# DVE and ACT in program order, and the softmax's last steps cut into other portions, in a two-layer cross-attention kernel

## The chip, the cores and the metric

The kernel runs on one core of one Trainium2 chip. Its engines work side by side, each through its own queue: TensorE (PE, with its weight loads as PEld), VectorE (DVE), ScalarE (ACT), GpSimd (POOL) and SyncE (SP). POOL and SP here mostly issue DMAs. The metric is the device time of one execution in microseconds (us), as the median of several runs. All data are float32.

## The reference, cut to what matters

Two layers of attention with a residual follow each other; the second takes the first one's output. Each has 8 batches of 100 queries, 640 channels and 20 heads of 32. The context has 722 tokens of 1024 channels per batch: 77 of text, and 645 of the second kind (`ip`). Text and `ip` have weights and a softmax of their own:

```
k, v       = text @ Wk, text @ Wv          # 77 tokens
k_ip, v_ip = ip @ Wk_ip, ip @ Wv_ip        # 645 tokens
out = softmax(q k^T / sqrt(32)) v + softmax(q k_ip^T / sqrt(32) + bias) v_ip * mask
x   = out @ Wo + bo + x
```

In the first layer there is no bias and no mask. In the second, the bias is 0.5 times a "semantic" score that all heads share (a softmax over whole rows of q and k of the text, carried over to the `ip` tokens), and the mask has one number for each query.

## The kernel before, in words

**Units.** The attention is cut into 80 units: 16 batches of a layer (u = 0 to 15, the second layer from 8 on) times 5 chunks of 4 heads (c = 0 to 4). `ORDER` (L41) runs through them batch by batch; for the last pair of batches (14 and 15) it takes chunks 0 and 2 of both, then 1 and 3 of both, then 4 of both. We write (14,3) for batch 14, chunk 3. Keys and values of the `ip` tokens are made two batches (a pair) at a time, by a Strassen-like scheme of seven products (`seven`, L179): PE makes a product in PSUM, ACT or DVE evicts it (L193, L202 on ACT; L198, L208, L213, L219, L224 on DVE). The sums that the scheme needs of the tokens (L232, L233, L527, L543, and L725, L726 for the last pair) and of the weights (L134 to L137) are made on DVE, a few on POOL. The keys and values go to DRAM, and come back for each unit.

**One unit.** `scores(u, c, 0)` makes the scores of 4 heads against the first 512 tokens on PE (L944), `scores(u, c, 1)` those of the other 210, the last 77 of them text. One PSUM tile of four banks holds either; it has no second buffer, so the next scores wait until the last ones have been read. Behind the scores stands the softmax:

- maxima on DVE: L953 in the first layer; in the second L960, which adds the bias, writes the result to `p` and takes the minimum of its negative in one instruction per head;
- exponentials with their sums on ACT (L968), and the text's maxima and its subtraction on DVE (L974, L976), with two small steps on the statistics (L979, L980);
- exponentials of the text and of the correction between the two halves on ACT (L983, L984);
- on DVE the sum over the text's columns (L985), two small steps (L986, L987), the reciprocal (L990) and the factors (L991);
- the scaling of the probabilities `p`: four instructions on ACT, one per head, for the first 512 columns (L997), and two on DVE for the rest (L1005 for the `ip` columns, L1001 for the text's).

One unit later, the probabilities are transposed on PE (`transposes`, L1030: six blocks j = 0 to 5 of four heads each; block 0 reads what L997 wrote), copied from PSUM (L1035 on ACT for j = 2 and 5, L1037 on DVE for the others), and multiplied with the values (`values`, L1052; the result's copy is L1056).

**Portions.** What stands behind the scores is not issued at once. `scores` puts it in portions into the list `later`. Each task of the production of keys and values that has a time of its own in the plan (the first number of its pair, over 0) is followed by one portion (`next_task`, L1220). `free_scores` (L930) issues those that must be out before the scores' PSUM tile is taken again (marked True), and the first transposes of a unit issue all that is left (L1025).

**What sets the order.** The production's tasks are spread over the units by a plan of estimated times (`production`, L1061, and `spread`, L1119), and the loop at L1253 interleaves them with scores, transposes, values, output pieces and query pieces. The whole is traced within `tc.manual_schedule(engines={PE})` (L1211): PE keeps the order in which the program issues its instructions. DVE, ACT and the queues of SP and POOL are ordered by the framework's scheduler, from estimates of its own. On each engine the instructions then run in the order that the build gave them. The start of the kernel (L415, text keys and values) is in a region of its own, where PE alone is pinned.

Of the kernel before, what the change touches and what calls it, by code (L numbers as in the profile page):

```python
# [44 lines left out]
def two_layer_xattn(  # L45
# [407 lines left out]
    def load_q(u):  # L453
        l, b = divmod(u, B)
        t = tpool.tile([P, NC_, S], F32, tag="q", name=f"q_{u}")
        nc.sync.dma_start(t, q_d[l][b // 2][:, b % 2])
        qs_[u] = t

    def load_vt(u):
        l, b = divmod(u, B)  # L460
        t = tpool.tile([NTAIL, C], F32, tag="vt", name=f"vt_{u}")
        nc.sync.dma_start(t[:NL], vl_d[l][b * NL : (b + 1) * NL, :])
        nc.sync.dma_start(t[NL:], vt_d[l][b * NT : (b + 1) * NT, :])
        vts[u] = t
# [459 lines left out]
    later = []  # L924

    def emit(n):
        for _ in range(n):
            later.pop(0)[1]()

    def free_scores():  # L930

        emit(max([i + 1 for i, (r, _) in enumerate(later) if r], default=0))

    def scores(u, c, part):
        k0, k1 = ((0, KA), (KA, NK))[part]
        free_scores()
        if part == 0:
            pr[u, c] = ppool.tile([S, 4, NK], F32, tag="p", name=f"p_{u}_{c}")

            stats[u, c] = stat.tile([S, 14, 4], F32, tag="st", name=f"st_{u}_{c}")  # L940
        sc = ps_sc.tile([P, 4, 512], F32, tag="sc", name=f"sc_{u}_{c}_{part}")
        for i in range(4):
            rows = slice(32 * i, 32 * i + 32)
            nc.tensor.matmul(  # L944
                sc[:S, i, : k1 - k0], lhsT=qs_[u][rows, c, :], rhs=ks[u, c][rows, k0:k1], start=True, stop=True
            )
        p, st, l = pr[u, c], stats[u, c], u // B
        n = min(k1, NI) - k0
        lo, f, rz, mul = st[:, 6, :], st[:, 7:9, :], st[:, 9:11, :], st[:, 11:13, :]

        def maxima(heads):
            if l == 0:
                nc.vector.tensor_reduce(  # L953
                    st[:, part, heads[0] : heads[-1] + 1], sc[:S, heads[0] : heads[-1] + 1, :n], AX.X, ALU.max,
                    negate=True,
                )
                return
            for i in heads:

                nc.vector.tensor_tensor_reduce(  # L960
                    out=p[:, i, k0 : k0 + n], in0=sc[:S, i, :n], in1=sems[u][:, k0 : k0 + n], scale=-1.0,
                    scalar=3.0e38, op0=ALU.add, op1=ALU.min, accum_out=st[:, part, i : i + 1],
                )

        def exponentials(heads):
            for i in heads:
                dst = p[:, i, k0 : k0 + n]
                nc.scalar.activation(  # L968
                    dst, dst if l else sc[:S, i, :n], AF.Exp, bias=st[:, part, i : i + 1],
                    scale=-1.0 if l else 1.0, accum_out=st[:, 3 + part, i : i + 1],  # L970
                )

        def text_maxima():
            nc.vector.tensor_reduce(st[:, 2, :], sc[:S, :, n:KB], AX.X, ALU.max, negate=True)  # L974

            nc.vector.tensor_tensor(  # L976
                p[:, :, NI:], sc[:S, :, n:KB], st[:, 2, :].unsqueeze(2).to_broadcast([S, 4, NT]), ALU.add
            )
            nc.vector.tensor_tensor(lo, st[:, 0, :], st[:, 1, :], ALU.min)  # L979
            nc.vector.tensor_tensor(f, lo.unsqueeze(1).to_broadcast([S, 2, 4]), st[:, 0:2, :], ALU.subtract)  # L980

        def text_exponentials():
            nc.scalar.activation(f, f, AF.Exp)  # L983
            nc.scalar.activation(p[:, :, NI:], p[:, :, NI:], AF.Exp)  # L984
            nc.vector.tensor_reduce(st[:, 5, :], p[:, :, NI:], AX.X, ALU.add)  # L985
            nc.vector.tensor_tensor(st[:, 3:5, :], st[:, 3:5, :], f, ALU.mult)  # L986
            nc.vector.tensor_tensor(st[:, 4, :], st[:, 3, :], st[:, 4, :], ALU.add)  # L987

        def factors():
            nc.vector.reciprocal(rz, st[:, 4:6, :])  # L990
            nc.vector.scalar_tensor_tensor(  # L991
                mul, f, mask_sb[:, l : l + 1], rz[:, 0:1, :].to_broadcast([S, 2, 4]), ALU.mult, ALU.mult
            )

        def scaled(heads):
            for i in heads:
                nc.scalar.activation(p[:, i, :KA], p[:, i, :KA], AF.Copy, scale=mul[:, 0, i : i + 1])  # L997

        def scaled_rest(text):
            if text:  # L1000
                nc.vector.tensor_tensor(  # L1001
                    p[:, :, NI:], p[:, :, NI:], rz[:, 1, :].unsqueeze(2).to_broadcast([S, 4, NT]), ALU.mult
                )
            else:
                nc.vector.tensor_tensor(  # L1005
                    p[:, :, KA:NI], p[:, :, KA:NI], mul[:, 1, :].unsqueeze(2).to_broadcast([S, 4, NI - KA]),
                    ALU.mult,
                )

        if part == 0:  # L1010
            maxima((0, 1))
            later.append((True, lambda: (exponentials((0, 1)), maxima((2, 3)))))
            later.append((True, lambda: exponentials((2, 3))))
        else:
            maxima((0, 1, 2, 3))
            later.append((True, lambda: (exponentials((0, 1, 2, 3)), text_maxima())))
            later.append((False, text_exponentials))
            later.append((False, lambda: (factors(), scaled((0, 1)), scaled_rest(False))))
            later.append((False, lambda: (scaled((2, 3)), scaled_rest(True))))

    pts = {}

# [185 lines left out]
        if n == len(ORDER) - 4:  # L1208
            last_out_weights()

    with tc.manual_schedule(engines={mybir.EngineType.PE}):  # L1211
        for _, f in pair_tasks(PAIRS[0]):
            f()
        load_q(0)
        load_vt(0)
        load_k(0, 0)
        todo = production()
        done = [0]

        def next_task():  # L1220
            todo[done[0]][2]()
            if todo[done[0]][0] and later:
                emit(1)
            done[0] += 1

        def make(until):
            while done[0] < len(todo) and todo[done[0]][1] < until:
                next_task()

        mark = [0]  # L1230

        def apart(until):

            while done[0] < len(todo) and todo[done[0]][1] < until and not any(
                t for t, _, _ in todo[mark[0] : done[0]]
            ):
                next_task()
            mark[0] = done[0]

        def between(n, a, b, small):  # L1240

            mark[0] = done[0]
            near = 0.4 if n < NC_ * LAST[0] + 6 else 0.1
            for i, (_, f) in enumerate(small):
                make(n + a + (b - a) * (i + 1) / (len(small) + 1))
                apart(n + b + near)
                f()
            make(n + b)
            apart(n + b + near)

        make(0.0)
        last = None
        for n, (u, c) in enumerate(ORDER):  # L1253
            at = small_work(n)
            loads(n)
            scores(u, c, 0)
            if n == len(ORDER) - 1:
                load_v(*last)
                load_v(u, c)
            between(n, 0.0, 0.4, at[0])  # L1260
            if last:
                transposes(*last, 0)
                transposes(*last, 1)
            between(n, 0.4, 0.6, at[1])
            if last:
                transposes(*last, 2)
                transposes(*last, 3)
            scores(u, c, 1)
            if n == NC_ * LAST[0] - 1:
                load_q(LAST[1])  # L1270
            between(n, 0.6, 0.8, at[2])
            if n < len(ORDER) - 2:
                load_v(u, c)
            if n + 1 < len(ORDER):
                load_k(*ORDER[n + 1])
            if last:
                transposes(*last, 4)
                transposes(*last, 5)
            between(n, 0.8, 1.0, at[3])
            if last:  # L1280
                values(*last)
            last = (u, c)
        last_out(0, [NC_ - 1])
        for j in range(6):
            transposes(*last, j, at_end=True)
        last_out_add(0)
        values(*last)
        last_out(1, [NC_ - 1])
        last_out_add(1)
# [46 lines left out]
```

## Time and profile before

| | |
|---|---|
| time, median of 3 runs | 2071.55 us (2071.48 to 2073.55) |
| time of the profiled execution | 2071.6 us |
| its span in the profile | 2069.8 us |
| mean granted TensorE clock | 0.998 |
| DMA, over the span | 255.35 MB, 123 GB/s |
| scaling on ACT, L997 | 320 instructions, 713 ns each |
| sum over the text's columns on DVE, L985 | 80 instructions, 469 ns each |
| maxima of the second layer on DVE, L960 | 320 instructions, 489 ns each (512 and 133 columns) |

The profiled execution took the median's time, and its span is 1.8 us less than its time; the rest lies around the program. The busy time of an engine says how full it is, not that it sets the end; for that one reads which engine waited for which (the view of waits) and the chain of work that ended last, followed back from the last instruction. The timeline lists instructions in the order of their start: start, duration, engine, line, operation, tiles and shape, how many in a row, and in brackets how long the engine had been idle and what ended that. PE's weight loads stand as PEld. Tile names come without their numbers, so that `p` may be that of any unit; which unit it is follows from the order.

### The profile page before, as it was taken

What the parts mean: (1) busy time and instruction counts of PE and PEld (TensorE: products, weight loads), DVE (VectorE), ACT (ScalarE), POOL (GpSimd) and SP (SyncE); (2) the same over time, 40 slices, a digit from 0 to 9 for tenths busy, and PEclk for the clock granted to TensorE, in tenths of its full rate; (3) what the DMA queues carried; (4) which work ended last, traced back from release to release, by engine and by line L of the source; (5) the groups of instructions that cost most, each with busy time, mean ns of one, the idle gap of its engine ahead of it and who ended that gap; (6) DMA issues with size and microseconds to landing.
All of it is one profiled execution on the core that took longest, in us unless ns stands there. A gap on an engine that the chain in (4) does not pass through costs nothing.

```text
span 2069.8 us, 38196 instructions
## 1 busy us (share of the span) xinstructions
PE 2043.5 (99%) x15122; PEld 1581.2 (76%) x15122; DVE 1074.8 (52%) x2789; ACT 799.6 (39%) x2271; POOL 309.9 (15%) x445
## 2 busy tenths in 40 slices
PE   9999999999999999999989999999999999999998
PEld 8676767677778777786778777787778778889787
DVE  2211322355554655455475555455555557777676
ACT  1001000244433434344333444435444445565576
POOL 3212312111111111010110111010111111111120
PEclk9999999999999999999999999999999999999999
DMA  9545313232424433262543533262434345545472
GB/s 327 155 132 171 97 56 105 88 107 71 129 83 131 129 113 91 81 179 65 160 133 103 147 105 106 72 178 75 115 89 134 90 133 151 158 133 140 121 211 74
DMA packets 302544, 255.35 MB, mean 123 GB/s; under 512 B 46686, under 2 KB 271378, under 8 KB 302366
## 3 DMA queue, kind: packets, MB, share of 16 engines
q1 hardware_dynamic: 280590, 184.48, 32.2%
q0 software_dynamic: 21776, 68.44, 9.5%
q8 instruction: 119, 1.95, 0.4%
q14 instruction: 59, 0.48, 0.1%
HBM read 183.93 MB, written 68.93 MB: 122 GB/s over the span
## 4 chain that ended last, share of the span: by engine, by line
PE 95%; DVE 2%; DMA 1%; ACT 1%; issue 1%; POOL 0%; SPq 0%; ACTq 0%; DVEq 0%
PE psv_a L597 8%; PE psv_d L597 8%; PE pspt L1030 8%; PE psk_d L625 6%; PE psk_a L625 6%; PE sc L944 6%; PE psk L563 5%; PE psv_e L597 4%; PE pv L1052 4%; PE psv_c L597 4%; PE psv_b L597 4%; PE psk_e L625 3%; PE psk_c L625 3%; PE psk_b L625 3%; PE pso L858 3%; PE psq L275 2%
## 5 line engine op out<-in xcount | busy, mean ns | idle before, releaser
L968 ACT ACTIVATE p<-sc,st 100x512 f32<-100x512 f32 (+1 forms) x320 | 166.4, 528 | 218.5 <-DVE st L953 218.2
L1037 DVE COPY pt<-pspt 128x400 f32<-128x400 f32 x319 | 175.5, 569 | 122.8 <-PE pspt L1030 116.6
L997 ACT ACTIVATE p<-p,st 100x512 f32<-100x512 f32 x320 | 208.5, 713 | 62.8 <-DVE st L991 62.7
L968 ACT ACTIVATE p<-p,st 100x512 f32<-100x512 f32 (+1 forms) x320 | 177.1, 555 | 132.3 <-DVE st L960 131.8
L1030 PEld LDWEIGHTS pspt<-ident,p 100*128 100x128 f32 (+1 forms) x1920 | 188.0, 137 | 42.1 <-issue 5.0
L1030 PE MATMUL pspt<-ident,p 100*128 100x100 f32 (+1 forms) x1920 | 211.0, 250 | 5.7 <-DVE res L863 2.4
L597 PE MATMUL psv_a<-wv,x 128*128 128x397 f32 (+1 forms) x560 | 185.0, 472 | 1.3 <-ACT vo L193 1.3
L646 POOL DMA_DIRECT2D k_d<-ko x140 | 99.5, 715 | 527.6 <-DVE ko L219 470.9
L597 PE MATMUL psv_d<-wv,s 128*128 128x320 f32 (+1 forms) x560 | 174.9, 455 | 0.0
L1035 ACT COPY pt<-pspt 128x400 f32<-128x400 f32 (+1 forms) x161 | 78.4, 487 | 227.7 <-PE pspt L1030 227.3
L953 DVE TENSOR_REDUCE st<-sc 100x2 f32<-100x1024 f32 (+1 forms) x120 | 126.3, 1052 | 59.4 <-ACT p L968 30.5
L597 PEld LDWEIGHTS psv_a<-wv,x 128*128 128x128 f32 x560 | 103.5, 190 | 63.7 <-issue 8.1
L960 DVE CUSTOM_DVE_ANT_0 p<-sc,sem 100x512 f32<-100x512 f32 (+1 forms) x320 | 139.7, 489 | 22.5 <-PE sc L944 22.3
L597 PEld LDWEIGHTS psv_d<-wv,s 128*128 128x128 f32 x560 | 103.4, 190 | 57.4 <-issue 5.5
L625 PE MATMUL psk_a<-x,wk 128*128 128x256 f32 (+1 forms) x672 | 137.2, 350 | 4.2 <-ACT ko L193 4.2
L944 PE MATMUL sc<-k,q 32*100 32x210 f32 (+1 forms) x1280 | 138.6, 502 | 0.8 <-ACT p L968 0.6
L625 PE MATMUL psk_d<-s,wk 128*128 128x256 f32 (+1 forms) x672 | 136.4, 348 | 0.0
L612 POOL DMA_DIRECT2D v_d<-vo x70 | 38.3, 548 | 642.4 <-DVE gst L587 317.5
L563 PE MATMUL psk<-x,wk 128*128 128x256 f32 (+1 forms) x560 | 132.0, 383 | 0.0
L625 PEld LDWEIGHTS psk_a<-x,wk 128*128 128x128 f32 x672 | 110.8, 192 | 24.7 <-issue 6.0
L563 PEld LDWEIGHTS psk<-x,wk 128*128 128x128 f32 x560 | 102.8, 189 | 25.7 <-issue 9.9
L625 PEld LDWEIGHTS psk_d<-s,wk 128*128 128x128 f32 x672 | 108.3, 189 | 17.5 <-issue 5.2
(209 smaller groups left out, 3234.5 us busy)
## 6 DMA issues: line engine op xcount, KB each, us to landing
x<-ip_t SPq DMA_DIRECT2D x84, 512.0 KB
k<-k_d SPq DMA_DIRECT2D x80, 322.5 KB
v<-v_d SPq DMA_DIRECT2D x80, 320.0 KB
v_d<-vo POOLq DMA_DIRECT2D x70, 320.0 KB, 2.5
k_d<-ko POOLq DMA_DIRECT2D x112, 128.0 KB, 4.3
x<-ip_t SPq DMA_DIRECT2D x22, 532.0 KB
o<-wo SPq DMA_DIRECT2D x35, 320.0 KB
q<-wq SPq DMA_DIRECT2D x20, 320.0 KB
```

The lines of the kernel that those rows point to most:

```text
L563: nc.tensor.matmul(ps[:, : 2 * n], lhsT=W["k", 4][:, k, :], rhs=x_all[:, at[j], :, k, :n], start=(k == 0), stop=(k == NCC - 1),)
L597: nc.tensor.matmul(ps[:, :m], lhsT=tokens(k)[:, :P], rhs=w[:, k, :], start=(k == 0 and not go_on), stop=(k == HK - 1), skip_group_check=True,)
L625: nc.tensor.matmul(ps[:, i * m : (i + 1) * m], lhsT=W["k", WHICH[which]][:, k, r * P : (r + 1) * P], rhs=tokens(k), start=(i == 0 and k == ...
L646: nc.gpsimd.dma_start(dst[:, :, r], ko[0][:, h, :, i, p0 : p0 + n])
L944: nc.tensor.matmul(sc[:S, i, : k1 - k0], lhsT=qs_[u][rows, c, :], rhs=ks[u, c][rows, k0:k1], start=True, stop=True)
L953: nc.vector.tensor_reduce(st[:, part, heads[0] : heads[-1] + 1], sc[:S, heads[0] : heads[-1] + 1, :n], AX.X, ALU.max, negate=True,)
L960: nc.vector.tensor_tensor_reduce(out=p[:, i, k0 : k0 + n], in0=sc[:S, i, :n], in1=sems[u][:, k0 : k0 + n], scale=-1.0, scalar=3.0e38, op0= ...
L968: nc.scalar.activation(dst, dst if l else sc[:S, i, :n], AF.Exp, bias=st[:, part, i : i + 1], scale=-1.0 if l else 1.0, accum_out=st[:, 3 ...
L997: nc.scalar.activation(p[:, i, :KA], p[:, i, :KA], AF.Copy, scale=mul[:, 0, i : i + 1])
L1030: nc.tensor.transpose(ps[:rows, i * S : (i + 1) * S], pr[u, c][:, i, j * P : j * P + rows], ident[:S, :S])
L1037: nc.vector.tensor_copy(dst, src)
L1052: nc.tensor.matmul(ps[32 * i : 32 * i + 32, :S], lhsT=lhs, rhs=pt[:rows, j, i * S : (i + 1) * S], start=(j == 0), stop=(j == 5),)
```

## The change

The diff in full:

```diff
@@ -982,11 +982,11 @@
         def text_exponentials():
             nc.scalar.activation(f, f, AF.Exp)
             nc.scalar.activation(p[:, :, NI:], p[:, :, NI:], AF.Exp)
+
+        def factors():
             nc.vector.tensor_reduce(st[:, 5, :], p[:, :, NI:], AX.X, ALU.add)
             nc.vector.tensor_tensor(st[:, 3:5, :], st[:, 3:5, :], f, ALU.mult)
             nc.vector.tensor_tensor(st[:, 4, :], st[:, 3, :], st[:, 4, :], ALU.add)
-
-        def factors():
             nc.vector.reciprocal(rz, st[:, 4:6, :])
             nc.vector.scalar_tensor_tensor(
                 mul, f, mask_sb[:, l : l + 1], rz[:, 0:1, :].to_broadcast([S, 2, 4]), ALU.mult, ALU.mult
@@ -1015,8 +1015,9 @@
             maxima((0, 1, 2, 3))
             later.append((True, lambda: (exponentials((0, 1, 2, 3)), text_maxima())))
             later.append((False, text_exponentials))
-            later.append((False, lambda: (factors(), scaled((0, 1)), scaled_rest(False))))
-            later.append((False, lambda: (scaled((2, 3)), scaled_rest(True))))
+            later.append((False, lambda: (factors(), scaled_rest(False))))
+            later.append((False, lambda: (scaled((0, 1)), scaled_rest(True))))
+            later.append((False, lambda: scaled((2, 3))))
 
     pts = {}
 
@@ -1208,7 +1209,7 @@
         if n == len(ORDER) - 4:
             last_out_weights()
 
-    with tc.manual_schedule(engines={mybir.EngineType.PE}):
+    with tc.manual_schedule(engines={mybir.EngineType.PE, mybir.EngineType.DVE, mybir.EngineType.Activation}):
         for _, f in pair_tasks(PAIRS[0]):
             f()
         load_q(0)
```

DVE and ACT keep the program's order from the first pair's production to the end. The second scores have five portions instead of four: exponentials and text maxima; the text's exponentials; the sum, the factors and L1005; two L997 with L1001; two L997. In the built program, no instruction is added or removed on any engine except waits. PE has its 8,549 matmuls in the same order. On DVE 2,094 of 2,789 instructions stand at another place than before, on ACT 862 of 1,623, on SP's queue 29 of 612, on POOL's 10 of 445; most of them move by a few places. The lines from L985 on shift by two in the new file (L985 to L987, L986 and L987 to L988 and L989), those of `transposes` and `values` by one; the text keeps the line numbers of before where it speaks of before.

## The prediction

> **What bounds the kernel now.** First the page's busy line and the chain that ended last.
>
> ```profile
> PE 2043.5 (99%) x15122; PEld 1581.2 (76%) x15122; DVE 1074.8 (52%) x2789; ACT 799.6 (39%) x2271; POOL 309.9 (15%) x445
> ...
> PE 95%; DVE 2%; DMA 1%; ACT 1%; issue 1%; POOL 0%; SPq 0%; ACTq 0%; DVEq 0%
> ```
>
> TensorE is busy for all but 26 us of 2069.8; DVE and ACT are half idle or more. Reordering them can therefore gain only what TensorE waits for. The view of waits on PE:
>
> ```profile
> PE psk_a L625 <- ACT ko L193: 4.2, 1, 4.2
> ...
> PE psk_c L625 <- DVE ko L198: 1.5, 1, 1.5
> ...
> PE psv_a L597 <- ACT vo L193: 1.3, 1, 1.3
> ...
> PE pspt L1030 <- ACT p L997: 0.3, 1, 0.3
> ```
>
> Beside a start of 4.5 us that the change does not touch, three waits stand out, and the transposes (pspt, L1030) wait for the scaled probabilities (p, L997) for 0.3 us in all. The DVE timeline about the 4.2 us one shows its cause:
>
> ```profile
> 1032.42 0.26 DVE L1056 COPY hs<-pv 128x100 f32<-128x100 f32 x1 [0.71 <-PE pv L1052]
> 1037.67 1.49 DVE L134 TENSOR_TENSOR wvt<-wv,wv 128x1280 f32<-128x1280 f32 x1 [4.98 <-DMA wv<-wvi]
> 1039.08 1.22 DVE L953 TENSOR_REDUCE st<-sc 100x2 f32<-100x1024 f32 x1
> ```
>
> The scheduler put a weight sum (L134) ahead of a score maximum (L953). The sum waited 4.98 us for its DMA, and everything behind it on DVE, then on ACT, then on PE, with it. Last, the timeline of all engines in unit (14,3), where unit (14,1) is finished:
>
> ```profile
> 1997.55 0.46 DVE L985 TENSOR_REDUCE st<-p 100x4 f32<-100x308 f32 x1
> ...
> 1998.88 2.56 ACT L997 ACTIVATE p<-p,st 100x512 f32<-100x512 f32 x4 [0.96 <-DVE st L991]
> ...
> 2000.22 1.12 PE L944 MATMUL sc<-k,q 32*100 32x512 f32 x8
> ...
> 2001.27 2.00 PE L775 MATMUL psk<-x,wk 128*128 128x256 f32 x8
> 2001.40 0.69 DVE L960 CUSTOM_DVE_ANT_0 p<-sc,sem 100x512 f32<-100x512 f32 x1 [0.79 <-PE sc L944]
> 2002.02 0.08 DVE L960 DVE_READ_ACCUMULATOR2_ANT st<- 100x1 f32 x1
> 2002.02 0.69 DVE L960 CUSTOM_DVE_ANT_0 p<-sc,sem 100x512 f32<-100x512 f32 x1
> ...
> 2003.10 0.85 PE L1030 MATMUL pspt<-ident,p 100*128 100x100 f32 x8
> ```
>
> Here the sum over the text columns (L985) starts 3.85 us before the next unit's maxima (L960), and the scaling (L997) ends at 2001.44, 1.9 us before PE reaches the fourth transpose (2003.36). That lead is what the scheduler's freedom buys, and what the change puts at stake.
>
> **The change part by part.** PE's order is the same in both built programs. On DVE and ACT no instruction is added or removed; 36 more wait instructions stand on PE (17 ns each by the row of such waits on ACT, 0.6 us at most, left out).
>
> *The late units.* A unit's portions go out one per timed task, and what is left goes out in one lump ahead of its transposes. There are now seven portions a unit instead of six. A middle pair gives 80 timed tasks to 10 units (8 each); the last pair gives 70 to 14.1 units, 14 to 4 and 6 to 2.05 (5, 3.5 and 3 each, L1105 to L1115). So in the late units the portion with L985 goes out after the next unit's first two maxima, and pinned, it stays there. In (14,3), L985 then starts when the second maximum ends, 2002.71. From L985 to L997 it is 1.33 us (1997.55 to 1998.88), the four L997 take 2.56: they end at 2006.60, and the fourth transpose, due 2003.36, is 3.2 late. Nothing covers it: PE's order is fixed and the next thing in it is the transpose.
>
> The same sum for each unit, with the row that now stands ahead of L985 or L997 (a maximum, or an eviction or copy of a later product) at its time in this trace: (13,4) 2.1; (14,0) 4.3; (14,2) 4.3; (15,0) 3.2; (15,2) 3.2; (14,1) 3.2; (14,3) 5.0; (15,1) 4.1; (15,3) 3.4; (14,4) 3.4. In (15,4) the text maxima (L974) fall behind the copy of (14,4)'s result, which ends at 2057.92; 1.52 us to L985 (2041.34 to 2042.86 in the unit before), 1.33 and 2.56 make 2063.3 against a fourth transpose at 2059.4: 3.9. **Together 40.** Both ends of most of these sums hang on PE's own order, so an earlier stall shifts both and heals nothing; I keep 30 to 44.
>
> *Units (11,3) to (13,3).* The same sum for nine of them gives 0.9 to 2.8 each, 16.7 in all. Here the blocker is mostly an ACT eviction (L193, L202) placed ahead of the scalings. A stall of PE gives ACT time to catch up for the following unit, so I take two thirds: **11** (4 to 17).
>
> *Six earlier units*, (0,3), (2,2), (4,2), (6,1), (6,2), (8,1): one copy of a PE product stands between the second and third L997, and PE goes from that product straight to the transposes. In (0,3): product at its end 482.62, copy L193 from 482.82 for 0.42, two L997 (0.64 apart, 0.71 long) to 484.5; the fourth transpose was due at 482.88: 1.6. **Six times 1.6 is 9.5** (0 to 9.5). The other 54 units have 4.6 to 14 us of lead and lose only lead.
>
> *Other DVE work now late.* The two sums for the last pair's first visit (L232, L233, from 1737.34) come behind two weight sums (1.22 each) and the second softmax's small chain that ends at 1739.4: they end near 1743.1, and PE wants them at 1740.1, 3 us. Three later visits have them behind maxima, 0.7 each. At seven output or query pieces the copy that frees the PSUM buffer (L1037) comes behind a maximum that waits for ACT, about 1 each. **12** (0 to 15).
>
> *What goes.* The weight sums are back behind the work that waits for PE: 4.2, 1.5 and 1.3 go, and with the first the half clock after it, seen here in the windows view (columns: stretch, length, PE, PEld, DVE, ACT, POOL busy, granted clock, DMA, GB/s):
>
> ```profile
> 1036.00:1042.00 6.00, 1.81 (x13) 1.62 (x13) 4.33 (x4) 1.67 (x5) 0.00 (x0) 0.93 0.51 173
> 1042.00:1046.00 4.00, 4.00 (x28) 4.00 (x27) 4.00 (x5) 0.97 (x4) 0.00 (x0) 0.67 0.00 0
> ```
>
> 0.67 over 4 us and 0.93 over 6 are 1.7 us of clock lost. **Minus 8.7** (0 to 8.7).
>
> *Clock.* New stalls may bring new such stretches at 1.7 us each. One followed a 4.2 us wait; the 1.5 and 1.3 us waits brought none; the stretch from 1930 to 1945, with 1.6 us idle in pieces, has a clock of 0.89, again 1.7 lost. Eleven late stalls of 2 to 5 us: 0 to 19; I take three, **5**, because the nearest rows are the single waits.
>
> [...]
>
> *Queues.* On SP 29 of 612 and on POOL 10 of 445 instructions move, by four and eight places at most. The x loads among them are issued two visits ahead, and the POOL sums are wanted only after the products from 207 to 238 us. I cost them at nothing; uncovered, the only landing on the chain is 6.4 us (wv at 1031.22).
>
> Sum: 40 + 11 + 9.5 + 12 - 8.7 + 5 = 69. The profiled execution took 2071.6, the median is 2071.55: **2141 us**.
>
> **Rivals.**
> *Only the late units lose* (the early ones have just enough lead, the sums and copies are absorbed): 40 + 11 - 9 + 0 = 42, about 2114, from 2100 to 2122. For it: a few tenths decide the six early places. Chance 0.16.
> *Every late stall also halves the clock*: 14 us more, 2155 to 2180. For it: the stretch from 1930 to 1945; against it: the waits of 1.5 and 1.3 us that cost no clock. Chance 0.13.
> *Faster:* the three waits and the half clock go, and the late chains arrive in time. 2071.6 - 8.7 is 2063. It decides at one point: the fourth L997 must end before the fourth transpose, so L985 may start later by no more than the lead, 1.9 us in (14,3); by the sum above it starts 5.2 later (1997.55 to 2002.71). It holds only if the portions with L985 go out ahead of those maxima, and the built order has them behind. Chance 0.05.
> *No change*, gains and losses even out within 0.2% (about what a measurement of this kernel can tell): 0.02. A pinning that does not hold is excluded, as the built program has the program's order on both engines.
>
> **How the numbers follow.** My forecast, 2122 to 2155, has 0.62, and 0.02 lies beyond 2180. The range reaches into both slower rivals: 2103 to 2168. Faster 0.05, same 0.02, slower 0.93.
>
> **What would show it.** In the waits on PE: "pspt <- ACT p L997" from 0.3 to about 60 us, most of it after 1930; psk_a and psk_c waits gone; DVE's 4.98 us wait for a DMA ahead of a sum gone. In the late timeline, L985's successor starts just after the second L960. In the windows, the clock stays at 1.00 up to the last units. I am wrong if the transposes' wait stays under 20 us, if it lies in the middle units, or if the lost time shows as a lower clock and not as idle PE.

## The result, and the profile after

The changed kernel takes 2157.02 us (median of six runs, 2155.59 to 2159.99); the kernel before took 2071.52 beside it. The ratio is 1.0414, with a 95% interval of 1.0401 to 1.0427: 85.5 us slower. The profiled execution took 2157.25 us, with a span of 2155.5.

The page of the profile after, in its busy line, its row of the TensorE clock (40 slices of 53.9 us) and its chain:

```profile
PE 2080.6 (97%) x15122; PEld 1600.7 (74%) x15122; DVE 1083.3 (50%) x2789; ACT 796.2 (37%) x2271; POOL 310.0 (14%) x445
...
PEclk9999999999999999999999999999999999999888
...
PE 92%; DVE 4%; ACT 3%; issue 1%; DMA 0%; SPq 0%; ACTq 0%; DVEq 0%
```

PE is idle for 74.9 us (2155.5 less 2080.6) where it was idle for 26.3: 48.6 more. Its busy time grew by 37.1 us with the same 15,122 instructions. So the lost time shows in two ways, and the clock row says where much of it lies: in the last three slices, 162 us, it falls below nine tenths. The waits on PE (us in total, times, longest):

```profile
PE pspt L1031 <- ACT p L997: 44.9, 72, 3.5
PE psvk_b L731 <- DVE sl L233: 5.4, 4, 3.1
PE psq L275 <- DMA wq<-wq: 4.5, 1, 4.5
PE pso L858 <- DVE pt L1038: 3.2, 3, 1.1
```

The transposes' wait for the scaling has risen from 0.3 us to 44.9. The waits named psk_a, psk_c and psv_a, 7.0 us together before, are gone. The timeline of the same place as in the prediction, unit (14,3), in which (14,1) is finished (start, duration, engine, line, and in brackets the idle time before and what ended it):

```profile
2054.26 1.12 PE L944 MATMUL sc<-k,q 32*100 32x512 f32 x8
...
2055.56 0.69 DVE L960 CUSTOM_DVE_ANT_0 p<-sc,sem 100x512 f32<-100x512 f32 x1 [0.89 <-PE sc L944]
...
2056.18 0.69 DVE L960 CUSTOM_DVE_ANT_0 p<-sc,sem 100x512 f32<-100x512 f32 x1
...
2056.79 0.47 DVE L987 TENSOR_REDUCE st<-p 100x4 f32<-100x308 f32 x1
...
2058.12 2.56 ACT L997 ACTIVATE p<-p,st 100x512 f32<-100x512 f32 x4 [0.36 <-DVE st L991]
...
2058.89 0.30 PE L1031 MATMUL pspt<-ident,p 100*128 100x100 f32 x1 [1.59 <-ACT p L997]
...
2059.51 0.30 PE L1031 MATMUL pspt<-ident,p 100*128 100x100 f32 x1 [0.31 <-ACT p L997]
```

The sum over the text's columns (now L987) stands behind the next unit's first two maxima (L960). It starts 2.53 us after the scores, where it started 2.67 ahead of them (1997.55 against 2000.22). L997 follows 1.33 us later and takes 2.56, and PE takes one transpose after each of the four: each L997 releases one.

The windows view of this stretch shows the second part of the loss (columns: stretch, length, PE, PEld, DVE, ACT, POOL busy, granted clock, DMA share, GB/s):

```profile
2054.13:2057.54 3.41, 3.18 (x28) 1.70 (x16) 2.20 (x8) 0.15 (x1) 0.00 (x0) 1.00 0.55 169
2057.54:2060.95 3.41, 1.13 (x5) 0.63 (x6) 2.75 (x8) 3.05 (x6) 1.07 (x2) 1.00 0.72 181
2060.95:2064.37 3.42, 3.42 (x12) 2.88 (x11) 1.15 (x2) 2.55 (x8) 0.00 (x0) 0.50 0.62 171
```

PE works for 1.13 of 3.41 us, and in the next 3.42 us it has work throughout and half the clock (0.50 granted). Before the last matmul such half-clock stretches fill 54.6 us, in twelve places; in the kernel before they fill 6.8 us, in two.

Since both kernels run the same 8,549 matmuls in the same order, the distance between the starts of two neighbours can be compared one by one. What grew is, by the tile that PE was held up at: transposes 63.8 us, matmuls inside half-clock stretches 15.3 (net of those that the kernel before has), the sums' products psvk_b 6.35, output and query pieces and second scores (pso, psq, sc) 10.4; psk_a, psk_c, psv_a and pskt_d give back 8.65. That is 87.2, against 85.7 us of span; 1.5 us of small differences either way stay unassigned. Where to put output pieces that themselves ran at half clock is a choice: counted with the clock, it lost about 17 us, and the pieces and second scores 8.5.

### The profile page after: what moved, and what is told of

It is laid out like the page before. It is cut to its first block, busy times and chain, and to the rows that moved or that the text cites. A ratio compares the mean times of both kernels' runs of the same rounds, so it can differ in the third digit from the quotient of the medians.

```text
span 2155.5 us, 38296 instructions
## 1 busy us (share of the span) xinstructions
PE 2080.6 (97%) x15122; PEld 1600.7 (74%) x15122; DVE 1083.3 (50%) x2789; ACT 796.2 (37%) x2271; POOL 310.0 (14%) x445
## 4 chain that ended last, share of the span: by engine, by line
PE 92%; DVE 4%; ACT 3%; issue 1%; DMA 0%; SPq 0%; ACTq 0%; DVEq 0%
PE psv_a L597 8%; PE psv_d L597 8%; PE pspt L1031 8%; PE sc L944 6%; PE psk L563 6%; PE psk_d L625 6%; PE psk_a L625 6%; PE pv L1053 4%; PE psv_e L597 4%; PE psv_c L597 4%; PE psv_b L597 4%; PE psk_e L625 3%; PE psk_b L625 3%; PE pso L858 3%; PE psk_c L625 2%; ACT p L997 2%
## 5 line engine op out<-in xcount | busy, mean ns | idle before, releaser
L1031 PE MATMUL pspt<-ident,p 100*128 100x100 f32 (+1 forms) x1920 | 231.3, 257 | 50.3 <-ACT p L997 44.9
L1031 PEld LDWEIGHTS pspt<-ident,p 100*128 100x128 f32 (+1 forms) x1920 | 195.0, 140 | 101.7 <-ACT p L997 60.5
L997 ACT ACTIVATE p<-p,st 100x512 f32<-100x512 f32 x320 | 208.5, 714 | 97.2 <-DVE st L991 97.1
L960 DVE CUSTOM_DVE_ANT_0 p<-sc,sem 100x512 f32<-100x512 f32 (+1 forms) x320 | 141.5, 490 | 27.3 <-PE sc L944 27.2
```

The lines of the kernel that those rows point to most:

```text
L960: nc.vector.tensor_tensor_reduce(out=p[:, i, k0 : k0 + n], in0=sc[:S, i, :n], in1=sems[u][:, k0 : k0 + n], scale=-1.0, scalar=3.0e38, op0= ...
L1031: nc.tensor.transpose(ps[:rows, i * S : (i + 1) * S], pr[u, c][:, i, j * P : j * P + rows], ident[:S, :S])
```

## The experiments

The theory: a pinned engine takes its instructions in the order in which the program issues them, and in the late units the softmax's last steps are issued in a lump behind the next unit's maxima; the place of issue costs the time. Rival A: holding the engines to any order costs it, wherever the portions are issued. Rival B: the new cut of the portions costs it. Rival C: the half clock is only a sign of the waiting and costs nothing by itself.

**1. Pinned, with the old portions.** The kernel before, with the change's last line alone:

```diff
-    with tc.manual_schedule(engines={mybir.EngineType.PE}):
+    with tc.manual_schedule(engines={mybir.EngineType.PE, mybir.EngineType.DVE, mybir.EngineType.Activation}):
```

> DVE and ACT pinned as in the change, but the four old portions, in which the sum over the text's columns goes out with the text's exponentials. Theory (a pinned queue runs the softmax's last steps where the program issues them, and the new portions issue them later): the late units keep a stall, but one portion's delay shorter, about 2 us less for each of 11 and some at the middle ones, and fewer half-clock stretches: about 2125 us (2112 to 2138). Rival A (any order but the scheduler's costs this much, whatever the portions): 2157. Rival B (the new portions cost, not the pinning): at or below the kernel before, 2063 to 2072.

Measured: 2132.43 us, ratio 1.0297 (1.0281 to 1.0312). The wait in question:

```profile
PE pspt L1030 <- ACT p L997: 29.6, 49, 3.0
```

61 of the 85 us come with the pinning alone. By the comparison of starts, transposes cost 43.9 us here against 63.8 in the changed kernel. The late units are nearly as late as there ((15,1) 4.7 in both, (15,4) 4.2 in both); I had expected each of them to be some 2 us less late, and the eleven together are only about 4 us less late than there. The old cut issues L985 a portion earlier, and it now runs ahead of the maxima, but the factors and the scalings still go out in the lump behind them. What the old portions spare is most of the early six and part of the middle units.

**2. The portions alone.** The changed kernel with PE alone pinned:

```diff
-    with tc.manual_schedule(engines={mybir.EngineType.PE, mybir.EngineType.DVE, mybir.EngineType.Activation}):
+    with tc.manual_schedule(engines={mybir.EngineType.PE}):
```

> The five new portions with PE alone pinned. Theory: the scheduler moves the steps forward again as before, so the time is that of before, 2071.5 us within 0.2%, with the 4.2 us wait of psk_a still there. Rival B (the portions themselves cost): 2100 or more.

Measured: 2071.08 us, ratio 1.0000 (0.9990 to 1.0009). The old wait is back:

```profile
PE psk_a L625 <- ACT ko L193: 4.3, 1, 4.3
```

Rival B falls. A scheduler that is free to reorder undoes the place of issue: only 69 places on DVE and 6 on ACT differ from the order of the kernel before. The cut costs 24.6 us only where the order is pinned (2157.0 less 2132.4).

**3. and 4. One engine at a time.** The changed kernel with PE and DVE pinned, then with PE and ACT:

```diff
-    with tc.manual_schedule(engines={mybir.EngineType.PE, mybir.EngineType.DVE, mybir.EngineType.Activation}):
+    with tc.manual_schedule(engines={mybir.EngineType.PE, mybir.EngineType.DVE}):
...
+    with tc.manual_schedule(engines={mybir.EngineType.PE, mybir.EngineType.Activation}):
```

> New portions, PE and DVE pinned, ACT left to the scheduler. Theory: the late units' chain begins on DVE (the sum behind the next maxima), so most of their 40 us stays; the six early waits behind an ACT copy (10 us) go, and half of the middle ones: about 2115 to 2135 us. Were ACT's order the cause: 2080 or less.

> New portions, PE and ACT pinned, DVE left to the scheduler. Theory: the scalings keep their late place in ACT's queue, behind evictions and exponentials, so the early six and the middle units keep their waits and the late ones a part: 2100 to 2125 us; the 4.2 us wait of psk_a behind the DVE weight sum may stay. Were DVE's order the only cause: 2072 to 2082.

Measured: DVE 2135.47 us, ratio 1.0311 (1.0295 to 1.0326), just above what was expected; ACT 2118.89, ratio 1.0231 (1.0216 to 1.0246). The same wait, first with DVE pinned, then with ACT:

```profile
PE pspt L1031 <- ACT p L997: 32.2, 54, 3.5
```

```profile
PE pspt L1031 <- ACT p L997: 28.0, 58, 3.0
```

With DVE pinned all late units stay late, and four of the early six are on time again (the other two are 1 us late). With ACT pinned the early six stay (1.3 to 1.7 each), and the late ones in part: (14,0) and (14,2) are on time, (15,1) is 4.7 late. That agrees with what the prediction named as blockers: maxima on DVE in the late units, a copy on ACT between two L997 in the early ones. The two do not add: 64 and 48 us alone, 85 together, since a unit whose chain is late by one queue is late once. I had thought that ACT alone might leave the psk_a wait. It left the cause and moved the wait: on DVE the weight sum still stands ahead of the maximum and waits 4.38 us for its DMA, and PE now waits behind it at psk_c (3.1 us of the last line below; its other 1.6 is a later wait that the kernel before has too, at 1.5).

```profile
1043.71 1.49 DVE L134 TENSOR_TENSOR wvt<-wv,wv 128x1280 f32<-128x1280 f32 x1 [4.38 <-DMA wv<-wvi]
1045.12 1.22 DVE L953 TENSOR_REDUCE st<-sc 100x2 f32<-100x1024 f32 x1
```

```profile
PE psk_c L625 <- DVE ko L198: 4.7, 2, 3.1
```

**5. and 6. Pinned, and issued earlier.** The changed kernel, with all portions of a unit issued ahead of the last unit's values, and so ahead of the next scores; first from the unit with n = 69, (13,4), on, then in every unit:

```diff
             between(n, 0.8, 1.0, at[3])
+            if n >= 69:
+                emit(len(later))
             if last:
                 values(*last)
```

```diff
             between(n, 0.8, 1.0, at[3])
+            emit(len(later))
             if last:
                 values(*last)
```

> The change, but from unit (13,4) on whatever is left of a unit's portions goes out ahead of the values' products, and so ahead of the next maxima in DVE's queue. Theory: most of the 39 us of waits in the last 11 units go, and with them most of the half-clock stretches (1.7 us each, ten more than before); the six early and the middle waits and the late sums stay: 2105 to 2120 us. Rival A (pinning as such costs): 2140 or more.

> The same in every unit: pinned DVE and ACT, but all portions out ahead of the values' products. Theory: nearly all waits of transposes for L997 go, below 10 us in all; what stays is the sums of the last pair (5 to 7 us), what goes is psk_a's, psv_a's and psk_c's wait with their half clock: 2070 to 2080 us, within some us of the kernel before. Rival A: 2120 or more.

Measured: the late units alone 2109.07 us, ratio 1.0185 (1.0166 to 1.0203); every unit 2079.94, ratio 1.0042 (1.0029 to 1.0056). Of 85.5 us, 48 and 77 come back, with both engines pinned as in the changed kernel. Rival A falls. The timeline of unit (14,3) in the first of the two:

```profile
2029.88 0.47 DVE L987 TENSOR_REDUCE st<-p 100x4 f32<-100x308 f32 x1 [1.89 <-ACT p L984]
...
2030.58 1.12 PE L944 MATMUL sc<-k,q 32*100 32x512 f32 x8
...
2031.22 2.56 ACT L997 ACTIVATE p<-p,st 100x512 f32<-100x512 f32 x4 [1.37 <-DVE st L991]
...
2033.47 1.02 PE L1031 MATMUL pspt<-ident,p 100*128 100x100 f32 x8
```

The sum is 0.7 us ahead of the scores again, and the transposes run as one group of eight with no bracket. In the second kernel the waits on PE begin with:

```profile
PE psvk_b L731 <- DVE sl L233: 7.2, 5, 3.1
PE psq L275 <- DMA wq<-wq: 4.4, 1, 4.4
PE pspt L1031 <- ACT p L997: 3.3, 11, 0.4
```

The transposes' wait is down to 3.3 us. By the starts of the matmuls, what keeps this kernel 8.5 us above the one before is the sums for the last pair (8.2) and transposes that are still held up (8.3 in all, 5.5 of it in the late units), less the waits that went.

**7. PE kept busy while it waits.** The changed kernel, with ten matmuls of the identity ahead of the first transposes of each unit of the last pair. They write PSUM that the transposes then overwrite, and add work that no result uses:

```diff
+        if j == 0 and u >= LAST[0]:
+            for _ in range(10):
+                nc.tensor.matmul(ps[:, :S], lhsT=ident, rhs=ident[:, :S], start=True, stop=True)
         for i in range(4):
             nc.tensor.transpose(
```

> The change, with ten idle matmuls (identity times identity, 128x100, some 0.22 us each, 2.2 us in all) ahead of the first transposes of the ten units of the last pair. They read nothing new, are overwritten by the transposes, and change no result. They lie in waits of 2.3 to 4.7 us. Theory (PE's idle time brings the half clock, and the half clock is on the path): most of the ten half-clock stretches after 1980 go and the time falls by 8 to 15 us, to 2142 to 2149. Rival C (the half clock costs nothing, since PE waits anyway): 2157, or a few us more where the idle matmuls outlast a wait.

Measured: 2146.89 us, ratio 1.0364 (1.0350 to 1.0378). More work, and 10.1 us less time. The windows of unit (14,3) here, in stretches of the same lengths:

```profile
2049.64:2053.05 3.41, 3.11 (x26) 2.79 (x24) 3.27 (x12) 2.40 (x5) 1.07 (x2) 1.00 0.49 112
2053.05:2056.47 3.42, 3.11 (x21) 2.67 (x22) 1.29 (x4) 3.35 (x9) 0.00 (x0) 1.00 0.86 244
```

The wait is filled (3.11 us busy of 3.41), and the full clock stays. Half-clock time before the last matmul falls from 54.6 us to 20.5. The stalls themselves did not shrink: by the starts of the matmuls, the transposes of the eleven late units are 39.3 us late here and 39.4 in the changed kernel. What shrank is what other matmuls lose inside half-clock stretches, by 11.2 us, where the span fell by 11.1 (2155.5 less 2144.4). Rival C falls: what the half clock cost was on the path.

**8. The gain without the loss.** The kernel before, with DVE pinned in four units only, n = 27 to 30, (5,2) to (6,0), about the place where the weight sum stood ahead of a maximum:

```diff
         for n, (u, c) in enumerate(ORDER):
+            with ExitStack() as pinned:
+                if 27 <= n <= 30:
+                    pinned.enter_context(tc.manual_schedule(engines={mybir.EngineType.PE, mybir.EngineType.DVE}))
...
```

The rest of the loop's body stands unchanged, one step further in, under this `with`.

> The kernel before, with DVE pinned in the four units (5,2) to (6,0) alone, where the weight sum stood ahead of the maximum. Theory: the 4.2 and 1.3 us waits go and with them one half-clock stretch (1.7): 2071.5 minus 5.5 to 7.2, about 2065 us, faster by 0.3%. Rival (the wait is DMA's in any order, or comes back elsewhere): 2071.5.

Measured: 2064.61 us, ratio 0.9970 (0.9959 to 0.9980). This beats both kernels, the one before by 6.8 us (2071.42 beside it). The waits on PE:

```profile
PE psq L275 <- DMA wq<-wq: 4.4, 1, 4.4
PE pspt L1030 <- DVE res L863: 2.4, 11, 0.6
PE pskt_d L316 <- issue: 2.2, 1, 2.2
PE psk_c L625 <- DVE ko L198: 1.8, 1, 1.8
```

Psk_a is gone, psv_a is at 0.6, and of the two half-clock stretches one is left. The wait at psk_c, which lies far behind the four units (1.5 us before, 1.8 here), stays.

## Why the prediction was right, and where its size was off

The direction, the mechanism and the range hold: 85.5 us slower against 69 forecast, 2157.0 in 2103 to 2168. The time is 2 us above the band of the forecast itself (2122 to 2155) and inside that of the second rival, "every late stall also halves the clock"; the range held because it reached into that rival. Term by term, measured by the starts of the matmuls:

| step | forecast, us | measured, us |
|---|---|---|
| late units, eleven stalls | +40 | +39.4 |
| units (11,3) to (13,3) | +11 | +12 |
| six early units | +9.5 | +10.0 |
| other DVE work | +12 | +16.8 |
| waits that go | -7.0 | -8.65 |
| clock, less the 1.7 that goes | +3.3 | +15.3 |

Two units that the forecast left out, (0,0) and (0,4), add 0.95 each.

- **Late units: right, by the sum given.** The prediction had 1.33 us from the sum to L997 and 2.56 for the four, counted from the end of the second maximum; the trace has 1.33 and 2.56. It put the fourth transpose for (14,1) 3.2 late; it was 3.3. Other units are off by up to 1.1 ((14,4): 2.3 against 3.4), and these misses cancel in the sum. Experiments 5 and 6 show that the place of issue is the cause. The view of waits has 44.9 us where about 60 was forecast: it counts idle time alone, and between two of these waits PE works 0.30 us on one transpose, where eight took 0.85 before.
- **Middle and early units: right.** The six lose 1.3 to 2.3 each (forecast 1.6). The two thirds that I allowed the middle nine came out at 12 of 16.7.
- **Other DVE work: too small.** The psvk_b wait of 3 us was forecast and is there (3.1). The output and query pieces and second scores cost 10.4; the second scores (2 times 1.3) were not in the forecast.
- **What goes: right.** Psk_a, psk_c and psv_a gave back about 7.7 us. The other 1.0 is pskt_d, a wait near the start that lies anywhere between 0.3 and 2.2 us in the ten traces. Experiment 8, which is spared psk_a, half of psv_a and one half-clock stretch without the losses, gains 6.8.
- **Clock: the term that was mis-sized.** The step was "I take three, **5**, because the nearest rows are the single waits". Ten more places appeared, and 47.8 us more of half clock (54.6 less 6.8). At half the rate that could cost 23.9 at most; 15.3 was lost (about 17 in the other count); PE waits in part of these stretches anyway (in the one from 2074.61 us it works for 1.29 of the first 3.41). Nine of the eleven late stalls brought one, so the second rival named what happened, and 0.13 was too little for it. I judged stalls by their length, from single cases in which PE was busy on both sides. In the late units one wait is followed by three more of 0.31 us, and PE's share of work over 3.41 us falls (1.13 us in the second line of the windows view above).
- Of the signs that would have shown me wrong, one came in part: lost time that shows as a lower clock and not as idle PE. The clock was to stay at 1.00 up to the last units; from 1960 us on its mean is 0.88.

## What to carry to other kernels

Pinning an engine makes the program's place of issue the schedule. Before doing it, look for the last step of each chain that the bound engine waits for, and for what the program issues ahead of it on that engine: here one added call, which issues the portions earlier, took back 77 of 85.5 us. Where the scheduler misplaces one instruction, pin the few units about it (four here, 0.3% faster), and leave it free elsewhere.

When stalls repeat on TensorE, ask also what the clock does behind them. Here half-clock time followed nine of the eleven late stalls, and the stalls alone gave too small a sum: 63.8 us on the transposes, and 15.3 more for the clock.

## What the runs showed of the hardware that was not expected

- **A stretch of half clock came behind a step in which PE was partly busy.** In the changed kernel's trace all half-clock stretches start at whole multiples of 3.413 us from one another (the second 47.79 us after the first, the third 58.03 after the second: 14 and 17 times that) and last 3.41 or 6.83 us, apart from the last, which lies behind the final matmul. In the step of 3.41 us ahead of each of the other twelve, PE was busy for 0.88 to 2.02 us, 26 to 59%.
- **The length of a stall did not decide.** The stall of 2.3 us at (14,4) brought a stretch, that of 3.0 at (15,3) none. The first lies in one such step, from 2122.40 us, in which PE was 59% busy (2.02 us of 3.41); the second is spread over two, from 2105.33 us, with 56 and 72% (1.91 and 2.46 us). So how the stalls lie in the steps does not explain the pair either. In this trace, from 40 us on, the full-clock steps that were followed by full clock were 56% busy or more. That does not settle it: in the kernel before, a step with 71% was followed by half clock (2.41 us, from 1935.49 us), and one with 55% was not (1.87 us, from 1723.86 us). What decides stays open.
- **Useless work paid.** Ten idle matmuls in each of ten waits took 10.1 us off.
